# When the turning in layer 3, the loads of x and one normalization are issued in a four-layer graph network kernel

## The chip, the cores and the metric

The kernel runs on one core of one Trainium2 chip, as one launch. The metric is the device time in microseconds (us) of that launch; the times below are medians of several runs. The engines are called by their short names: PE is TensorE, DVE is VectorE, ACT is ScalarE, POOL is GpSimd and SP is SyncE. Each takes its own instructions from its own queue, in the order in which the program put them there.

## The reference, cut to what matters

There are 128 graphs of 64 nodes with 256 features each, and one 64x64 adjacency. Four layers follow each other, each on a normalized copy of x and each added back to x. All is float32.

```python
def reference(x, adj, ...):                    # x: 128 x 64 x 256
    # layer 0: two graph convolutions, then an LSTM over windows of 1, 2, 3 and 4 nodes
    h = max(layernorm(x), 0)
    h = relu(adj @ (h @ Wg0 + bg0)); h = relu(adj @ (h @ Wg1 + bg1))
    for p in (1, 2, 3, 4):
        h[:, p-1::p] = lstm_last(Wih[p-1], Whh[p-1], windows of p nodes of h)
    x = x + h
    # layer 1: attention with four heads under the mask of adj
    h = max(layernorm(x), 0); x = x + attention(h @ W, adj)
    # layer 2: adjacency, linear 256->512, batch norm, relu, linear 512->256, batch norm
    h = max(layernorm(x), 0); x = x + batchnorm(relu(batchnorm(A_hat @ h @ W1.T)) @ W2.T)
    # layer 3: three convolutions with adj * adj, 256 -> 512 -> 1024 -> 256
    h = max(layernorm(x), 0); w = adj * adj
    return x + w @ (relu(w @ (relu(w @ (h @ W1)) @ W2)) @ W3)
```

## The kernel before, in words

The 8192 tokens (a token is one node of one graph) are cut into 16 groups of 512. `xs[g]` is the residual x of group g with tokens on partitions: four tiles `x0` to `x3` that stay from the start, eight parts of the tiles `x_for_h0` and `x_for_h1` (groups 4 to 11) that take the room of two tiles of h when the LSTM has no more use for it, and four tiles for groups 12 to 15.

Products of matrices are done by a scheme with seven block products instead of eight. `sums` and `differences` (L206 and L218) make its operands, mostly on DVE. `seven` issues the seven products on PE: products 1, 5, 6 and 7 first, whose results ACT copies to p1 and p5 (L173, L174) and DVE adds to them (L176, L177); then products 2, 3 and 4, with the output blocks made by DVE (L185, L189) and one of them by POOL, the sum at L180.

**The LSTM** runs over windows of p nodes, for p = 1 to 4. For p = 4 the last pair of units is j = 2; there each step t = 1, 2, 3 is done for i = 0 and i = 1 by `next_step`, with two sets of gates (`gate_set`, the products at L560). `output` ends a step: tanh of the cell on ACT (L593), and a multiply with the output gate on DVE (L595 for the state, L601 in the last step, where the result goes back to h). Beside these steps h goes back to x, in pieces numbered by `slot = 2 t + i - 2`: `turn_nodes` transposes 32x32 blocks on DVE (L270) and puts them to DRAM tensors y with SP's queue (L275); `x_for` loads the input x of four groups (`load_x`, L58, SP); `add_turned` (L283) adds y to `xs[g]` with an accumulating transfer that POOL issues. Pieces for which there is no room in the LSTM are turned and added in the attention.

When step t = 3, i = 0 has been issued, the program normalizes `xs[0]` (`ln_relu`): statistics on DVE (L92, L94, L95), the inverse root on POOL (L96), the shift on DVE (L98) and four activations on ACT (L111). `transposed` then turns it with eight transposes on PE (L127), and `features` copies the result to `hT` (L294) and makes its differences (L298, L302, L303).

**The attention** goes over the groups one by one. In group g `queries_keys` makes q and k with the seven products (L872; the sum of k is L180 on POOL), `scores` are at L919, `add_output` multiplies on DVE (L980) and adds to x on POOL (L983), `normalized` prepares group g + 2 (L853 to L859), and `shifts_made[g]` is its last POOL instruction (L859) for group g + 1.

**Layer 3** goes over the groups too: `first_weights` (L1408), `second_mix` (L144, with copies L154), `second_weights` (L1444), `start` for the next group, `third_weights` (L1489), and `last_mix` (L1510) of the group before with its residual add (L1529). Beside them the output of layer 2, which is held feature by feature in `outs`, goes back to x: `normalize(g)` applies the second batch norm on ACT (L1280) or DVE (L1282), and `bring` takes groups in turn: the first eight are turned on PE (`to_residual`), the others by `turn_over`, with two transposes on DVE (L1317) and eight puts to DRAM by SP (L1321); `add_over` adds the DRAM tensor z to `xs[g]` with an accumulating transfer from POOL (L1330).

The order on each engine comes from the order in the program and from a list scheduler that may move independent work; `tc.issue_after(instruction)` ties what is issued inside it behind that instruction.

Of the kernel before, what the change touches and what calls it, by code (L numbers as in the profile page):

```python
# [10 lines left out]
ALU = mybir.AluOpType  # L11
# [9 lines left out]
NG = NTOK // GN  # L21
# [3 lines left out]
NK = PER  # L25
# [13 lines left out]
def adj_preln_kernel(ctx: ExitStack, tc: tile.TileContext, x_in, adj, vec, bg0, bg1,  # L39
                     wg0, wg1, wih, whh, wqkv, w1t, w2t, l3w1, l3w2, l3w3, out):  # L40
    nc = tc.nc
# [119 lines left out]

    HN = GN // 2

    def seven(products, banks, p1, p5, out, end, parts=lambda b: [b]):

        ps = banks  # L170
        for i, p in zip((1, 5, 6, 7), ps):
            products[i](p, True)
        nc.scalar.copy(p1, ps[0])  # L173
        copied = nc.scalar.copy(p5, ps[1])  # L174

        nc.vector.tensor_tensor(p1, p1, ps[2], ALU.add)  # L176
        added = nc.vector.tensor_tensor(p5, p5, ps[3], ALU.add)  # L177

        def finish():
            nc.gpsimd.tensor_tensor(out=out[1][1], in0=p1, in1=p5, op=ALU.add)  # L180
            end(1, 1, None)
            products[2](ps[0], False)
            end(0, 0, ps[0])
            products[3](ps[1], False)
            nc.vector.tensor_tensor(out[0][1], p1, ps[1], ALU.add)  # L185
            end(0, 1, None)
            products[4](ps[3], False)
            for to, p, q in zip(*(parts(b) for b in (out[1][0], p1, ps[3]))):
                last = nc.vector.tensor_tensor(to, p, q, ALU.add)  # L189
# [116 lines left out]
    with tc.tile_pool(name="lw", bufs=5) as lw:  # L306
# [220 lines left out]
        with tc.tile_pool(name="back", bufs=1, reuse_waits="tile") as back_pool, \  # L527
# [62 lines left out]
            def output(t, p, u, gate_o, th):  # L590

                x_of, cell, hid = u
                nc.scalar.activation(th, cell, AF.Tanh)  # L593
                if t < p - 1:
                    nc.vector.tensor_tensor(hid, gate_o, th, ALU.mult)  # L595
                else:
                    for blk in range(2):
                        o, h = (
                            v[:, :, blk, :].rearrange("p c (k b) -> p c k b", b=HB) for v in (gate_o, th)
                        )  # L600
                        nc.vector.tensor_tensor(x_of(t, blk), o, h, ALU.mult)  # L601

            behind = []

# [63 lines left out]
            def next_step(t, p, n, u, ws, last_sum=None):  # L668

                x_of, cell, hid = u  # L670
                tt = dp.tile([P, 4, 2, 256], F32, tag="diff", name="diff")
                ts = [tt[:, i, :, 0:n] for i in range(4)]
                wide = [d.rearrange("p c (k b) -> p c k b", b=HB) for d in ts]
                x1, x2 = (x_of(t, blk) for blk in range(2))
                h1, h2 = (hid[:, :, blk, :] for blk in range(2))
                nc.vector.tensor_tensor(wide[0], x2, x1, ALU.subtract)
                nc.vector.tensor_tensor(
                    wide[2], h2.rearrange("p c (k b) -> p c k b", b=HB), x2, ALU.subtract
                )
# [12 lines left out]
                output(t, p, u, gate_o, gate_g)  # L692

            def first_blocks(wi, room, behind=None):

# [28 lines left out]
            for p, nk in ((1, 8), (2, 8), (3, 7), (4, 8)):  # L724
# [7 lines left out]
                for j in range(0, len(units), 2):  # L732
# [22 lines left out]
                            nc.vector.tensor_tensor(wdiff, wqk[0][0], wqk[1][0], ALU.subtract)  # L755
                    for t in range(1, p):
                        for i, u in enumerate(two):
                            next_step(t, p, n, u, ws, last_sum if (j, t, i) == (0, 1, 0) else None)

                            if p == 4 and j == 2:  # L760
                                slot = 2 * t + i - 2
                            if p == 4 and j == 2 and t == p - 1:
                                for x_of_group in range(4 + 2 * i, 6 + 2 * i):
                                    add_turned(x_of_group)
                                if i == 0:
                                    x_for(1)
                            if p == 4 and j == 2 and t < p - 1:
                                if slot == 0:
                                    room = keep.tile([P, 2, TN, 2, 32], F32, tag="arena", name="turned")
                                for part in range(2 * slot, 2 * slot + 2):  # L770
                                    turn_nodes(
                                        part,
                                        room[:, part % 3] if part % 3 < 2 else back_pool.tile(
                                            [P, TN, 2, 32], F32, tag="hc", name="turned"
                                        ),
                                    )()
                                if slot == 2:
                                    x_for(0)
                                if slot > 1:
                                    for x_of_group in range(2 * slot - 4, 2 * slot - 2):  # L780
                                        add_turned(x_of_group)
                            if p == 4 and j == 2 and t == p - 1 and i == 0:

                                h = back_pool.tile([P, GT, D], F32, tag="hc", name="h")
                                ln_relu(xs[0], h)
                                hTs = keep.tile([P, 2, 2, GN], F32, tag="arena", name="hT")
                                hT = features(transposed(h))

# [54 lines left out]
    with tc.tile_pool(name="att", bufs=2, reuse_waits="tile") as ap_:  # L843
# [151 lines left out]
        for g in range(NG):  # L995
# [36 lines left out]
            if g == 1:  # L1032

                eT, turned = turn(e)
            if NK < g <= NG - NK:
                with tc.issue_after(shifts_made[g]):
                    add_turned(g + NK - 1)
            if g + 1 < NG:
                hT = features(transposed(h))
            if g == 0:  # L1040
# [268 lines left out]
    room = w_att[:, :, 512:1024]  # L1309
    turned_over = []  # L1310

    def turn_over(g):

        o = outs[g // 2][:, 2 * (g % 2) : 2 * (g % 2) + 2, :]
        y = turned_pool.tile([GN, D], F32, tag=f"z{g}", name=f"z{g}")
        for c in range(2):
            nc.vector.transpose(room[:, c], o[:, c, :])  # L1317
# [110 lines left out]
    def second_weights(m1, room):  # L1428
# [38 lines left out]
            end()  # L1467
        return h2, last

    def third_weights(h2, parts=lambda b: [b]):  # L1470


# [7 lines left out]
            )  # L1480
            for i in range(4)
        ]
        sums(nc.vector, *act[0], *act[1], *ss)

        def product(w, b):
            def issue(ps, first):
# [65 lines left out]
    for g in range(NG + 1):  # L1552
        if g == 0:
            bring(0, 3)
        if g < NG:

            m1 = arena(ar_right)
            h1, summed = first_weights(a, m1)
            if g == 0:
                with tc.issue_after(summed):  # L1560
                    finish_start()
            bring(3 if g == 0 else 1, 2 if g == 0 else 1)
        if s3 is not None:
            pss = [bank((P, 2, D)) for _ in range(2)]
            if g == NG:
# [14 lines left out]
        if g < NG:  # L1580
            h2, behind = second_weights(m1, h1)
            if g == 0:
                with tc.issue_after(behind):
                    for b, pss in later:
                        add_back(b, pss)
            bring(1, 1)
            if g + 1 < NG:
                a = start(g + 1, behind)
            if g == NG - 1:
                s3 = third_weights(h2, lambda b: [b[:, t] for t in range(2)])  # L1590
            else:
                s3 = third_weights(h2)


# [50 lines left out]
```

## Time and profile before

| | us |
|---|---|
| median of three runs | 2455.6 (2454.81 to 2458.61) |
| the profiled execution | 2455.04 |
| its span, first to last instruction | 2453.3 |
| PE busy | 2429.1 |
| DVE busy | 1538.6 |
| ACT busy | 1127.0 |
| POOL busy | 464.5 |

The time of an execution is a little longer than its span; every place in the trace is told in us from the span's start. PE, the busiest engine, stands still for 24.2 us of the span, and the granted clock of PE is 1.00 in the profile's record. The layers lie so: the convolutions of layer 0 to about 163, the LSTM to 1208, the attention to about 1425, layer 2 to about 1670, layer 3 to the end.

### The profile page before, as it was taken

The page shows a single profiled execution, that of the slowest core. Times are in us where ns is not written, and L with a number is a line of the kernel's source. Part 1 is how long each engine was busy: PE and PEld are TensorE (multiplying, and loading weights), DVE is VectorE, ACT ScalarE, POOL GpSimd, SP SyncE. Part 2 cuts the span into 40 slices and gives each one's busy share as a digit, 9 for nine tenths or more (in the row PEclk, how much of TensorE's full clock was granted, in tenths as well). Part 3 has the DMA queues.
Part 4 walks back from the last instruction along what each step waited for, and adds up shares of the span by engine and source line. Part 5 has one row for each costly group of instructions (what it writes and reads, how often), then busy time and mean ns, then how long its engine had stood idle before and what let it go on. Part 6 is the DMA issues. An engine that isn't in the chain of part 4 may idle for free.

```text
span 2453.3 us, 46571 instructions
## 1 busy us (share of the span) xinstructions
PE 2429.1 (99%) x19564; PEld 2072.5 (84%) x19564; DVE 1538.6 (63%) x2768; ACT 1127.0 (46%) x2026; POOL 464.5 (19%) x400
## 2 busy tenths in 40 slices
PE   9999999999999999999999999999999999999999
PEld 6678888889999998888888864487888898898888
DVE  6668866656566576585599886476655445454544
ACT  4557754444445343344455566564333323333332
POOL 4431211111111111122134331033111111111110
PEclk9999999999999999999999999999999999999999
DMA  3200000001000000173046410011322000000000
GB/s 128 93 2 1 1 18 1 1 1 35 1 1 1 1 1 1 18 128 75 14 88 120 79 34 1 1 61 23 64 48 42 10 10 19 10 10 10 18 10 18
DMA packets 161586, 73.20 MB, mean 30 GB/s; under 512 B 104416, under 2 KB 157792, under 8 KB 161376
## 3 DMA queue, kind: packets, MB, share of 16 engines
q1 hardware_dynamic: 147712, 56.82, 9.4%
q0 software_dynamic: 12672, 12.58, 3.4%
q8 instruction: 154, 2.52, 0.4%
q10 hardware_dynamic: 992, 0.82, 0.1%
q14 instruction: 56, 0.46, 0.1%
HBM read 40.84 MB, written 20.97 MB: 25 GB/s over the span
## 4 chain that ended last, share of the span: by engine, by line
PE 87%; DVE 7%; ACT 3%; issue 1%; POOL 1%; DMA 0%; SPq 0%; DVEq 0%; POOLq 0%; ACTq 0%
PE ps L560 40%; PE ps L1444 15%; PE ps L1489 8%; PE ps L822 4%; PE ps L144 4%; PE ps L872 3%; PE ps L1408 2%; PE ps L503 2%; PE ps L479 2%; PE ps L1201 2%; PE ps L1252 2%; PE ps L894 1%; ACT arena L229 1%; POOL arena L180 1%; PE ps L955 1%
## 5 line engine op out<-in xcount | busy, mean ns | idle before, releaser
L1444 PE MATMUL ps<-arena 128*128 128x256 f32 x1792 | 392.9, 380 | 2.7 <-DVE arena L206 1.4
L560 PE MATMUL ps<-diff,s 128*128 128x256 f32 (+1 forms) x1824 | 393.5, 371 | 0.9 <-DVE diff L680 0.9
L1444 PEld LDWEIGHTS ps<-arena 128*128 128x128 f32 x1792 | 338.0, 190 | 57.4 <-issue 6.9
L560 PEld LDWEIGHTS ps<-diff,s 128*128 128x128 f32 x1824 | 345.9, 190 | 33.8 <-issue 1.6
L574 ACT ACTIVATE gates<-gates,lbias 128x512 f32<-128x512 f32 (+5 forms) x426 | 244.3, 621 | 205.9 <-DVE gates L185 149.1
L180 POOL TENSOR_TENSOR gates<-p 128x512 f32<-128x512 f32 (+1 forms) x115 | 149.0, 1296 | 881.6 <-DVE p L177 830.8
L560 PE MATMUL ps<-h,w 128*128 128x256 f32 (+1 forms) x1028 | 241.0, 371 | 0.0
L560 PE MATMUL ps<-diff,w 128*128 128x256 f32 (+1 forms) x1040 | 238.8, 371 | 1.9 <-DVE p L177 1.9
L560 PEld LDWEIGHTS ps<-diff,w 128*128 128x128 f32 x1040 | 197.3, 190 | 20.5 <-DVE p L177 2.3
L560 PEld LDWEIGHTS ps<-h,w 128*128 128x128 f32 x1028 | 195.0, 190 | 19.2 <-issue 0.5
L574 ACT ACTIVATE gates<-ps,lbias 128x256 f32<-128x256 f32 (+3 forms) x213 | 91.6, 476 | 242.2 <-PE ps L560 242.1
L180 POOL TENSOR_TENSOR arena<-arena 128x256 f32<-128x256 f32 (+1 forms) x73 | 82.5, 1130 | 583.0 <-DVE arena L177 553.3
L229 ACT ACTIVATE arena<-arena 128x512 f32<-128x512 f32 (+1 forms) x160 | 88.7, 582 | 196.4 <-POOL arena L180 105.7
L1489 PE MATMUL ps<-arena 128*128 128x128 f32 x1280 | 149.9, 276 | 0.0
L185 DVE TENSOR_TENSOR gates<-p,ps 128x512 f32<-128x512 f32 (+1 forms) x115 | 76.2, 663 | 114.0 <-PE ps L560 113.8
L1489 PEld LDWEIGHTS ps<-arena 128*128 128x128 f32 x1280 | 145.6, 192 | 1.2 <-issue 0.2
L185 DVE TENSOR_TENSOR arena<-arena,ps 128x256 f32<-128x256 f32 (+1 forms) x73 | 43.5, 596 | 152.8 <-PE ps L1444 84.0
L560 PE MATMUL ps<-state,w 128*128 128x256 f32 (+1 forms) x512 | 116.1, 370 | 0.9 <-ACT p L173 0.8
L189 DVE TENSOR_TENSOR gates<-p,ps 128x512 f32<-128x512 f32 (+1 forms) x115 | 76.5, 666 | 64.4 <-PE ps L560 63.8
L176 DVE TENSOR_TENSOR p<-p,ps 128x512 f32<-128x512 f32 (+1 forms) x131 | 86.7, 662 | 47.5 <-PE ps L560 46.9
L560 PE MATMUL ps<-state,s 128*128 128x256 f32 (+1 forms) x512 | 115.8, 369 | 0.0
L822 PE MATMUL ps<-arena,w 128*128 128x512 f32 x256 | 114.3, 599 | 0.0
(207 smaller groups left out, 4016.6 us busy)
## 6 DMA issues: line engine op xcount, KB each, us to landing
x<-in_x SPq DMA_DIRECT2D x19, 512.0 KB, 4.7
y<-turned SPq DMA_DIRECT2D x64, 128.0 KB, 3.8
v<-vt SPq DMA_DIRECT2D x128, 64.0 KB, 2.2
w<-in_wih SPq DMA_DIRECT2D x4, 1024.0 KB, 8.0
x_for_h<-in_x SPq DMA_DIRECT2D x8, 512.0 KB, 7.0
x<-y POOLq DMA_DIRECT2D x8, 512.0 KB, 8.2
x_for_h<-y POOLq DMA_DIRECT2D x8, 512.0 KB, 6.5
z<-w SPq DMA_DIRECT2D x64, 64.0 KB, 2.0
```

Of the source, the lines that this page charges most:

```text
L144: last = nc.tensor.matmul(pss[b][half * 64 : half * 64 + 64, c, t, :], lhsT=src[rows, t, col : col + 64], rhs=a2[rows, :], start=True, sto ...
L176: nc.vector.tensor_tensor(p1, p1, ps[2], ALU.add)
L180: nc.gpsimd.tensor_tensor(out=out[1][1], in0=p1, in1=p5, op=ALU.add)
L185: nc.vector.tensor_tensor(out[0][1], p1, ps[1], ALU.add)
L189: last = nc.vector.tensor_tensor(to, p, q, ALU.add)
L229: nc.scalar.activation(o, o, func)
L560: nc.tensor.matmul(ps[:, r], lhsT=wc[:, j, :], rhs=bc, start=first and r == 0 and c == 0, stop=True, skip_group_check=True,)
L574: nc.scalar.activation(o, ps, func, bias=lbias[:, col : col + 1])
L822: nc.tensor.matmul(ps, lhsT=w1[:, c, m * P : (m + 1) * P], rhs=a[:, 2 + c, :], start=(c == 0), stop=(c == 1),)
L872: nc.tensor.matmul(ps[:, r, :], lhsT=w[:, r * P : (r + 1) * P], rhs=x, start=first and r == 0, stop=True, skip_group_check=True,)
L1444: nc.tensor.matmul(ps[:, r, :], lhsT=w[:, c, col : col + P], rhs=b[:, c, :], start=first and r == 0 and c == 0, stop=c == 1, skip_group_ch ...
L1489: nc.tensor.matmul(ps[:, t, :], lhsT=w[:, c, t * P : (t + 1) * P], rhs=b[:, c, :], start=first and t == 0 and c == 0, stop=c == 3, skip_gr ...
```

## The change

Four edits are made together.

1. In the LSTM's last pair of units, x's additions are spread: one group's addition in each of slots 2, 3 and 4 and two in slot 5, each tied behind POOL's last sum at L180. The loads of x for four groups each come in slots 3 and 4, behind all puts of y.
2. The normalization of `xs[0]` is tied behind the last multiply of step t = 3, i = 0 (`stepped`).
3. The additions for groups 5, 6 and 7 go to groups 1, 2 and 3 of the attention.
4. In layer 3 the two transposes of a group that is turned over, and the normalization of a later one, are tied behind the differences of `second_weights`, or behind the last sum of `third_weights`; `add_over` is tied behind POOL's last sum. The call of `bring` after `first_weights` stays for group 0 alone, and one after `third_weights` takes its place for the others.

`sums_on_pool` is the list of POOL's sums, to which `seven` appends; all else of `seven`, `add_turned`, `normalize` and `third_weights` is as before.

```diff
+    sums_on_pool = []
+    ADDED_BESIDE = ((), (), (0,), (1,), (2,), (3, 4))
+    def summed_last():
+        return sums_on_pool[-1]
...
         def finish():
-            nc.gpsimd.tensor_tensor(out=out[1][1], in0=p1, in1=p5, op=ALU.add)
+            sums_on_pool.append(
+                nc.gpsimd.tensor_tensor(out=out[1][1], in0=p1, in1=p5, op=ALU.add).ins
+            )
...
-                            if p == 4 and j == 2 and t == p - 1:
-                                for x_of_group in range(4 + 2 * i, 6 + 2 * i):
-                                    add_turned(x_of_group)
-                                if i == 0:
-                                    x_for(1)
-                            if p == 4 and j == 2 and t < p - 1:
...
-                                for part in range(2 * slot, 2 * slot + 2):
+                                for part in range(2 * slot, min(2 * slot + 2, 8)):
...
-                                if slot == 2:
-                                    x_for(0)
-                                if slot > 1:
-                                    for x_of_group in range(2 * slot - 4, 2 * slot - 2):
+                                for x_of_group in ADDED_BESIDE[slot]:
+                                    with tc.issue_after(summed_last()):
                                         add_turned(x_of_group)
+                                if slot > 2:
+                                    if slot < 5:
+                                        x_for(slot - 3)
                             if p == 4 and j == 2 and t == p - 1 and i == 0:
...
-                                ln_relu(xs[0], h)
+                                with tc.issue_after(stepped):
+                                    ln_relu(xs[0], h)
...
-            if NK < g <= NG - NK:
+            if 0 < g <= NG - NK:
                 with tc.issue_after(shifts_made[g]):
-                    add_turned(g + NK - 1)
+                    if g < 4:
+                        add_turned(g + NK)
+                    elif g > 4:
+                        add_turned(g + NK - 1)
...
-    def turn_over(g):
+    def turn_over(g, behind):
...
-        for c in range(2):
-            nc.vector.transpose(room[:, c], o[:, c, :])
+        with tc.issue_after(behind):
+            for c in range(2):
+                nc.vector.transpose(room[:, c], o[:, c, :])
...
-    def bring(n, ahead):
+    def bring(n, ahead, behind=None):
         nonlocal ready, brought
-        add_over()
         for _ in range(n):
+            if turned_over:
+                with tc.issue_after(summed_last()):
+                    add_over()
             if brought < ready:
-                (to_residual if brought < NG // 2 else turn_over)(brought)
+                if brought < NG // 2:
+                    to_residual(brought)
+                else:
+                    turn_over(brought, behind)
                 brought += 1
         for _ in range(ahead):
             if ready < NG:
-                normalize(ready, on_scalar=range(2 if ready < 5 else 1))
+                with tc.issue_after(behind) if behind else nullcontext():
+                    normalize(ready, on_scalar=range(2 if ready < 5 else 1))
                 ready += 1
...
-            bring(3 if g == 0 else 1, 2 if g == 0 else 1)
+            if g == 0:
+                bring(3, 2)
...
-            bring(1, 1)
+            bring(1, 1, behind)
...
                 s3 = third_weights(h2)
+                if g:
+                    bring(1, 1, third_summed)
```

More of the change, by code (lines that the diff above doesn't have):

```diff
@@ L594, in output @@
                 if t < p - 1:
-                    nc.vector.tensor_tensor(hid, gate_o, th, ALU.mult)
+                    last = nc.vector.tensor_tensor(hid, gate_o, th, ALU.mult)
                 else:
@@ L600, in output @@
                         )
-                        nc.vector.tensor_tensor(x_of(t, blk), o, h, ALU.mult)
+                        last = nc.vector.tensor_tensor(x_of(t, blk), o, h, ALU.mult)
+                return last.ins
             behind = []
@@ L691, in next_step @@
                 nc.vector.tensor_tensor(cell, cell, gate_i, ALU.add)
-                output(t, p, u, gate_o, gate_g)
+                return output(t, p, u, gate_o, gate_g)
             def first_blocks(wi, room, behind=None):
@@ L757, in adj_preln_kernel @@
                         for i, u in enumerate(two):
-                            next_step(t, p, n, u, ws, last_sum if (j, t, i) == (0, 1, 0) else None)
+                            stepped = next_step(
+                                t, p, n, u, ws, last_sum if (j, t, i) == (0, 1, 0) else None
+                            )
                             if p == 4 and j == 2:
                                 slot = 2 * t + i - 2
-                            if p == 4 and j == 2 and t == p - 1:
-                                for x_of_group in range(4 + 2 * i, 6 + 2 * i):
-                                    add_turned(x_of_group)
-                                if i == 0:
-                                    x_for(1)
-                            if p == 4 and j == 2 and t < p - 1:
                                 if slot == 0:
                                     room = keep.tile([P, 2, TN, 2, 32], F32, tag="arena", name="turned")
-                                for part in range(2 * slot, 2 * slot + 2):
+                                for part in range(2 * slot, min(2 * slot + 2, 8)):
                                     turn_nodes(
@@ L1468, in second_weights @@
         return h2, last
+    third_summed = None
     def third_weights(h2, parts=lambda b: [b]):
@@ L1482, in third_weights @@
         ]
-        sums(nc.vector, *act[0], *act[1], *ss)
+        nonlocal third_summed
+        third_summed = sums(nc.vector, *act[0], *act[1], *ss)
         def product(w, b):
```

## The prediction

> **What bounds the kernel now.** I read the busy times first, then TensorE's waits, then the timeline where those waits lie. Page, parts 1 and 4 (busy time; shares of the chain that ended last):
>
> ```profile
> PE 2429.1 (99%) x19564; PEld 2072.5 (84%) x19564; DVE 1538.6 (63%) x2768; ACT 1127.0 (46%) x2026; POOL 464.5 (19%) x400
> PE 87%; DVE 7%; ACT 3%; issue 1%; POOL 1%; DMA 0%; SPq 0%; DVEq 0%; POOLq 0%; ACTq 0%
> ```
>
> TensorE (PE) is the bound: idle for 2453.3 - 2429.1 = 24.2 us in all. The change alters no matmul and no order on PE, so it can win part of these 24.2 us, or add idle time to them. PE's waits (releaser: total, times, longest) and the timeline (start, us, engine, line, operation, [idle before it <- releaser]) at the three places that it touches:
>
> ```profile
> PE ps L560 <- DVE p L177: 1.9, 1, 1.9
> PE ps L919 <- POOL k L180: 1.8, 3, 0.6
> ...
> 1081.48 5.41 POOL L283 DMA_DIRECT2D x<-y  x4
> 1090.20 0.43 DVE L92 BATCH_NORM_STATS2 st<-x 128x6 f32<-128x256 f32 x1 [4.31 <-DMA x<-y]
> 1096.87 1.99 PE L560 MATMUL ps<-diff,w 128*128 128x256 f32 x8 [1.94 <-DVE p L177]
> ...
> 1181.58 1.89 PE L560 MATMUL ps<-diff,w 128*128 128x256 f32 x8
> 1183.31 1.04 PE L127 MATMUL ps<-ident,h 128*128 128x128 f32 x8
> 1184.18 1.89 PE L560 MATMUL ps<-h,w 128*128 128x256 f32 x8
> ```
>
> At 1090 VectorE (DVE) stands 4.31 us at the first statistics of x0, which wait for its accumulating transfer; the LSTM's adds queue behind, and PE loses 1.94 us. At 1183 the transposes of h (x0 normalized early, around 1100) stand on PE between the last product of step t=3, i=0 and the first of i=1, and PE does not stop. In layer 3 a turning transpose is in the way:
>
> ```profile
> 1739.89 0.71 DVE L1317 STREAM_TRANSPOSE w<-arena 128x512 f32<-128x512 f32 x1 [0.74 <-ACT arena L1280]
> 1741.78 3.69 PE L1444 MATMUL ps<-arena 128*128 128x256 f32 x16 [0.74 <-DVE arena L154]
> ```
>
> DVE waits for ScalarE's normalization, transposes, and so copies the mix (L154) late.
>
> **What the Trainium skill says.** "TensorE: Matmul & The Clock Gate", Part 2, step-by-step: "The MATMULs themselves stay in program order". The trace agrees: 1183.31 stands where the program has it. So a transpose that waits holds back everything behind it. Same page, Part 1, what's actually happening: after an idle window of about 3.4 us the array's clock halves until about 3.4 us of work have passed. The granted clock is 1.00 all through here, but at the span's start 14 matmuls of 128x128 took 3.35 us (239 ns each), while layer 3's L1489 of that width take 5.62/48 = 117 ns. "GPSIMD Engine Reference", 1. Specifications: the SBUF interfaces are shared with VectorE, with contention for DVE instructions with two SBUF inputs. The trace agrees (DVE L298: 0.69 us alone, 1.94 us under a GpSimd sum; shown below).
>
> **The change, part by part.** Lines are those of the kernel before.
>
> (a) End of the LSTM, the wait at 1090. The additions to x0 to x4 now go one by one behind GpSimd's (POOL's) sums of slots 2 to 5, and SyncE's loads of x4 to x7 pass behind the last eight puts of y. Each added transfer costs POOL about 0.85 to 1.3 us of issuing in gaps of 9 to 11 us (idle before L180); I take 0. x0 is added behind the second sum of t=2, i=0 (1130.9 in the timeline), and the statistics move to about 1190: the wait goes. Gain 1.9 us; bounds 1 and 1.94. Late next could be a transpose waiting for its put, but the puts now share the DMA engines with fewer transfers.
>
> (b) The normalization of x0 tied behind `stepped`. This is the term that decides. `stepped` is the last multiply of L601 in step t=3, i=0. The statistics, the inverse root, ScalarE's (ACT) four activations and then PE's eight transposes all come after it; the transposes keep their place in PE's queue, ahead of all products of step i=1. From PE's last product to h there is now one serial chain. Its first half is shown by step i=1, its second by a normalization in layer 3:
>
> ```profile
> 1208.56 0.69 DVE L189 TENSOR_TENSOR gates<-p,ps 128x512 f32<-128x512 f32 x1 [1.04 <-PE ps L560]
> 1213.76 1.29 DVE L601 TENSOR_TENSOR h<-gates 128x512 f32<-128x512 f32 x2 [1.18 <-ACT gates L593]
> ...
> 1746.27 1.40 DVE L92 BATCH_NORM_STATS2 st<-x 128x6 f32<-128x256 f32 x4
> 1749.49 2.08 ACT L111 ACTIVATE arena<-x,nmr,rstd 128x256 f32<-128x256 f32 x4 [3.40 <-DVE nmr L98]
> ```
>
> PE could go on at 1208.36 there, and L601 ended at 1215.05: 6.7 us. From statistics to the end of L111: 1751.57 - 1746.27 = 5.3 us. The new order puts one statistic of x1 between (0.34 us, most of the others beside POOL's root): 5.6. Six of the eight transposes run between the activations; the last two cost 2 x 0.13, with about 0.25 for the first weight load. h is thus complete at 1183.3 + 6.7 + 5.6 = 1195.6, and the next product starts at about 1196.1 instead of 1184.2: **11.9 us** of PE time, with nothing else in the queue to fill it. Bounds 11.0 (a quicker hand-over) and 12.6. Queued behind: all of step i=1. The copies of hT, its differences and x1's statistics then stand before L173 and L176, but those need PE's products, over 1.9 us later.
>
> (c) The clock after (b). Twelve us almost without matmuls are long enough for the page's throttle; 4 us at half rate cost 2.0 us. Bounds: 0 (the eight transposes keep it up) and 4 (the slow start lasted about 8 us). I take **2.0**.
>
> (d) Additions to x5, x6, x7 move into attention groups 1, 2, 3, behind `shifts_made`. POOL's new order in groups 2 and 3 is transfer, two output adds (L983), then the sum of k (L180), where before k came first. Groups 5 and 6 of the kernel before show both orders: windows (stretch, us, then busy times) of group 5 and group 6, and group 6's timeline:
>
> ```profile
> 1284.62:1298.47 13.85, 13.83 (x190) 11.92 (x189) 12.92 (x28) 7.98 (x15) 6.16 (x6) 1.00 0.74 137
> 1298.47:1313.56 15.09, 14.26 (x190) 12.10 (x189) 14.14 (x28) 8.18 (x15) 6.25 (x6) 1.00 0.78 157
> ...
> 1303.04 1.75 POOL L180 TENSOR_TENSOR k<-p 128x512 f32<-128x512 f32 x1
> 1303.41 1.94 DVE L298 TENSOR_TENSOR hT<-hT 128x512 f32<-128x512 f32 x1 [0.81 <-ACT hT L294]
> ```
>
> The late k falls under L298, and the group lasts 15.09 - 13.85 = 1.24 us longer. Twice: **2.5 us**. Group 1 has no output adds and k is ready 2.8 us before L919 needs it: 0. Bounds 0 and 2.6.
>
> (e) Layer 3. A group's period, between the starts of L1408 in the chain of waits, is 48.83, 48.37, 48.43 and 47.89 us for groups 1 to 4, which hold the turning, and 47.60 for most later ones: 3.1 us over the floor. Both transposes (2 x 0.70) and the normalization (0.5) now stand behind the differences, or behind the third sums, and no longer before L154. What queues behind them is L176/L177 of the second weights, whose products wait only after 14 us of others, and those of the third, needed at 1778.6 where they would end at about 1776.2. POOL's transfer follows its puts by half a group, so no wait is added there. Gain **3.1 us**; bounds 1.0 and 3.4. SyncE's 64 puts only change places.
>
> Sum: -1.9 + 11.9 + 2.0 + 2.5 - 3.1 = +11.4. The profiled execution took 2455.04 us (span 2453.3 and 1.74 around it), 0.56 below the median 2455.6 of three. 2455.04 + 11.4 = **2466.4 us**.
>
> **The rivals.** *Not slower: PE is not held at the transposes.* If h were ready by 1183.3 (an x0 normalized beside earlier steps, as before), (b) and (c) drop out: 2455.04 - 1.9 - 3.1 + 2.5 = 2452.5, or 2450.0 if (d) costs nothing as well. The point from which it decides: the chain in (b) would have to start 12 us earlier. For it: the kernel before did so. Against: the tie names the multiply itself, and DVE and ACT hold the chain in that order.
>
> *A heavier stall.* The clock stays low as long as at the start (+2) and ScalarE or DVE hand over late (+0.7): 2469.1. For it: the slow first 8 us. Against: step i=1 is dense, the start was not.
>
> *VectorE becomes the bound in layer 3.* The 1.9 us put ahead of L176 reach PE in the two turns of about four groups: 8 x 1.9 = 15.2 us and the 3.1 not won: 2484.7. Against: DVE is busy 24.2 of 48 us in such a group, and the slack named in (e).
>
> **How the numbers follow.** Forecast as worked out, 0.75; heavier stall 0.13; no stall 0.09; layer 3 bound 0.03. Low ends: 2455.04 + 11.0 + 0 + 0 - 1.94 - 3.4 = 2460.7. High ends: 12.6 + 4 + 2.6 - 1 - 1.0 = +17.2, 2472.2. The range 2460 to 2472 takes these in and leaves out the no-stall case and layer 3. A measurement tells about 0.2%, 4.9 us, from no change: slower by more 0.91, within 0.06 (most of the no-stall case), faster by more 0.03.
>
> **What would show each step.** (b) L127's first transposes waiting for ACT h L111, a total near 12 us in PE's waits, at about 1183; L92 behind L601. (c) L560's spacing near 430 ns for some 4 us afterwards. (a) No wait of PE on L177. (d) Groups 2 and 3 near 15.1 us, DVE L298 near 1.9. (e) Groups 1 to 4 of layer 3 at 47.6. The prediction is wrong if PE passes the transposes without an idle stretch of several us.

## The result, and the profile after

The changed kernel takes **2465.78 us** in the median of six runs (2465.19 to 2466.86); the kernel before takes 2455.11 beside it (2454.81 to 2458.61). The ratio is 1.0042, with a 95% interval of 1.0029 to 1.0055: slower by some 10.7 us. The prediction was 2466.4. The profiled execution has a span of 2464.0 us, 10.7 more than the 2453.3 of before.

Lines of the file have moved, so these are the same places under new numbers: the LSTM's products are L568 (L560 before), its last multiply L609 (L601), the sum on POOL L187 (L180), the second addition to p5 L183 (L177), the scores L926 (L919), the first weights of layer 3 L1419 (L1408). L92, L111 and L127 keep theirs. Parts 1 and 4 of the page of after:

```profile
PE 2431.4 (99%) x19564; PEld 2074.0 (84%) x19564; DVE 1544.5 (63%) x2768; ACT 1128.6 (46%) x2026; POOL 463.3 (19%) x400
PE 88%; DVE 7%; ACT 3%; POOL 1%; issue 1%; DMA 0%; DVEq 0%; POOLq 0%; ACTq 0%
```

PE executes the same 19564 matmuls and is busy 2.3 us longer, although no work was added to it: some of the products ran slower. It is idle for 2464.0 - 2431.4 = 32.6 us instead of 24.2. PE's waits in after, longest totals first (releaser: total, times, longest):

```profile
PE ps L127 <- ACT h L111: 11.0, 4, 10.5
PE ps L926 <- POOL k L187: 3.1, 5, 0.7
```

One wait of 10.5 us for the normalized x0 is new, the wait for the late k has grown from 1.8 to 3.1, and that of the LSTM's products for p is gone. The timeline of after at the new wait (start, us, engine, line, operation, [idle before it <- releaser]):

```profile
1179.69 1.89 PE L568 MATMUL ps<-diff,w 128*128 128x256 f32 x8
1186.82 1.29 DVE L609 TENSOR_TENSOR h<-gates 128x512 f32<-128x512 f32 x2 [1.18 <-ACT gates L601]
1188.04 1.40 DVE L92 BATCH_NORM_STATS2 st<-x 128x6 f32<-128x256 f32 x4
1191.45 2.07 ACT L111 ACTIVATE h<-x,nmr,rstd 128x256 f32<-128x256 f32 x4 [4.66 <-DVE nmr L98]
1192.10 2.16 PE L127 MATMUL ps<-ident,h 128*128 128x128 f32 x8 [10.52 <-ACT h L111]
1194.06 3.58 PE L568 MATMUL ps<-h,w 128*128 128x256 f32 x8
1197.47 5.35 PE L568 MATMUL ps<-diff,s 128*128 128x256 f32 x24
```

The chain stands there line by line: last product, multiply, statistics behind it, activations, transposes. The eight products at 1194.06 take 3.58 us where the eight at 1179.69 took 1.89. The windows of after (stretch, its length, then busy us of PE, PEld, DVE, ACT and POOL, then the granted clock, the DMA share and GB/s) say why; the last three are attention groups 2, 3 and 4:

```profile
1181.40:1194.06 12.66, 2.14 (x10) 1.35 (x9) 8.08 (x25) 4.58 (x8) 2.25 (x3) 0.60 0.22 34
1194.06:1197.47 3.41, 3.41 (x10) 2.69 (x9) 1.54 (x3) 1.07 (x2) 0.00 (x0) 0.50 0.00 0
...
1254.74:1269.92 15.18, 14.15 (x189) 11.94 (x188) 14.23 (x28) 8.07 (x15) 6.32 (x7) 1.00 0.62 103
1269.92:1285.11 15.19, 14.15 (x189) 11.94 (x188) 14.25 (x28) 8.06 (x15) 6.33 (x6) 1.00 0.65 111
1285.11:1298.96 13.85, 13.70 (x189) 11.73 (x188) 12.90 (x28) 7.83 (x15) 4.95 (x5) 1.00 0.49 103
```

The clock is 0.50 for 3.41 us after the wait. Groups 2 and 3 now last 15.2 us, where group 4, without an addition, lasts 13.85. POOL and DVE in group 2:

```profile
1259.40 1.75 POOL L187 TENSOR_TENSOR k<-p 128x512 f32<-128x512 f32 x1
1259.69 2.02 DVE L306 TENSOR_TENSOR hT<-hT 128x512 f32<-128x512 f32 x1 [0.81 <-ACT hT L302]
```

In layer 3, the chain of waits of after shows the starts of groups 1 to 4 (start, us, what):

```profile
1745.84 3.47 PE ps L1419 x16
1793.44 3.47 PE ps L1419 x16
1841.05 3.47 PE ps L1419 x16
1888.65 3.47 PE ps L1419 x16
```

Their distances are 47.60, 47.61 and 47.60 us; before they were 48.83, 48.37 and 48.43. In the second weights, PE's waits of before for the copies of the mix (L154, 0.7 on DVE and 0.6 on ACT) and for the operands' sums (L206, 1.4) are gone from the list of after.

Since PE's matmuls stand in one order in both traces, the start of each can be subtracted from that of its counterpart. The difference changes at few places, and these are the terms of the prediction (a plus is time lost):

| place (us) | term | predicted | measured |
|---|---|---|---|
| start of the span | none | 0 | +0.3 |
| 1094 to 1100 | (a) wait at 1090 | -1.9 | -2.2 |
| 1182 to 1194 | (b) wait at the transposes | +11.9 | +11.8 |
| 1194 to 1197 | (c) half clock | +2.0 | +1.7 |
| 1248 to 1285 | (d) late k in groups 2 and 3 | +2.5 | +2.8 |
| 1690 to the end | (e) layer 3 | -3.1 | -3.7 |
| sum | | +11.4 | +10.7 |

### The profile page after: what moved, and what is told of

Read it like the earlier page. It is cut to its first block, busy times and chain, and to the rows that moved or that the text cites. A ratio compares the mean times of both kernels' runs of the same rounds, so it can differ in the third digit from the quotient of the medians.

```text
span 2464.0 us, 46585 instructions
## 1 busy us (share of the span) xinstructions
PE 2431.4 (99%) x19564; PEld 2074.0 (84%) x19564; DVE 1544.5 (63%) x2768; ACT 1128.6 (46%) x2026; POOL 463.3 (19%) x400
## 4 chain that ended last, share of the span: by engine, by line
PE 88%; DVE 7%; ACT 3%; POOL 1%; issue 1%; DMA 0%; DVEq 0%; POOLq 0%; ACTq 0%
PE ps L568 41%; PE ps L1455 16%; PE ps L1503 8%; PE ps L829 4%; PE ps L144 4%; PE ps L1419 2%; PE ps L511 2%; PE ps L487 2%; PE ps L879 2%; PE ps L1211 2%; PE ps L1262 2%; PE ps L901 1%; ACT arena L237 1%; POOL arena L187 1%; DVE hT L306 1%
## 5 line engine op out<-in xcount | busy, mean ns | idle before, releaser
L568 PE MATMUL ps<-diff,s 128*128 128x256 f32 (+1 forms) x1824 | 393.5, 371 | 0.9 <-DVE diff L689 0.9
L568 PEld LDWEIGHTS ps<-diff,s 128*128 128x128 f32 x1824 | 346.1, 190 | 33.9 <-issue 1.6
L187 POOL TENSOR_TENSOR gates<-p 128x512 f32<-128x512 f32 (+1 forms) x115 | 149.2, 1297 | 892.5 <-DVE p L183 841.6
L568 PE MATMUL ps<-h,w 128*128 128x256 f32 (+1 forms) x1028 | 242.7, 373 | 0.0
L568 PE MATMUL ps<-diff,w 128*128 128x256 f32 (+1 forms) x1040 | 238.7, 370 | 0.0
L568 PEld LDWEIGHTS ps<-diff,w 128*128 128x128 f32 x1040 | 197.4, 190 | 18.2
L568 PEld LDWEIGHTS ps<-h,w 128*128 128x128 f32 x1028 | 196.2, 191 | 19.6 <-issue 0.5
L187 POOL TENSOR_TENSOR arena<-arena 128x256 f32<-128x256 f32 (+1 forms) x73 | 81.8, 1120 | 580.4 <-DVE arena L183 550.7
L568 PE MATMUL ps<-state,w 128*128 128x256 f32 (+1 forms) x512 | 116.1, 370 | 0.9 <-ACT p L179 0.8
L568 PE MATMUL ps<-state,s 128*128 128x256 f32 (+1 forms) x512 | 115.8, 369 | 0.0
```

Source lines behind the costliest of these rows:

```text
L568: nc.tensor.matmul(ps[:, r], lhsT=wc[:, j, :], rhs=bc, start=first and r == 0 and c == 0, stop=True, skip_group_check=True,)
```

## The experiments

The theory to test is that sum: one tie makes (b) and (c) and also wins (a), the moved additions make (d), and the edits of layer 3 win (e), each by itself. The rivals are that the long wait only covers others that would come elsewhere, that the half clock is a slow start of another kind, and that the gain in layer 3 depends on what came before it. The rivals named in the experiments are those of the expectation that stands above each. Line numbers shift by a few from kernel to kernel: the scores of L926 are L931 in busy_wait, the LSTM's products of L568 are L570 in later_transposes. The experiments ran in three comparisons, on three chips, and every ratio is to the runs of the kernel before on the same chip. Its medians there, against 2455.11 above, were 2456.02 us (for tie_alone, no_tie, adds_in_lstm and layer3_alone), 2457.04 (for tie_earlier, later_transposes, busy_wait and best_later) and 2455.55 (for busy_wait_64 and best_earlier).

### The tie alone, put into the kernel before (tie_alone)

The core of the edit; the other lines hand the last multiply on as `stepped`.

```diff
-                                ln_relu(xs[0], h)
+                                with tc.issue_after(stepped):
+                                    ln_relu(xs[0], h)
```

> The kernel before with only the tie of x0's normalization behind the last multiply of step t = 3, i = 0. My theory: the tie alone makes the stall at the transposes (+11.8) and the half clock (+1.7), and takes away the wait of the statistics for x0's transfer at 1090 (-2.2), since they are issued 100 us later: 2455.1 + 11.3 = 2466.4 us, between 2465 and 2468. Rival 1 (the stall needs the new order of additions and loads as well): about 2455, within 1. Rival 2 (the gain of 2.2 at 1090 comes from the spread additions and not from the later statistics): 2468.6, with the wait of PE L560 for DVE p L177 still there.

Measured: 2466.46 us, ratio 1.0039 (1.0027 to 1.0052), span 2464.7. PE's waits in this kernel begin with

```profile
PE ps L127 <- ACT h L111: 10.7, 2, 10.5
```

and its wait for L177 is gone. Against the trace of before the matmuls gain 2.2 us at 1094 and lose 13.6 from 1182 to 1197. So one edit holds (b) and (c), and (a) with them: the wait at 1090 goes because the statistics come 100 us later, whether x's additions are spread or not. Both rivals fall.

### The changed kernel without the tie (no_tie)

```diff
-                                with tc.issue_after(stepped):
-                                    ln_relu(xs[0], h)
+                                ln_relu(xs[0], h)
```

> The changed kernel without the tie of x0's normalization behind the last multiply of step t = 3, i = 0; all else as changed. The scheduler then puts the statistics of x0 (L92) beside an earlier step, while PE's order stays the same. My theory (the stall at the transposes is the whole loss, terms b and c): h is ready before PE comes to L127, PE does not stop there, and the 11.8 + 1.7 us go: 2465.8 - 13.5 = 2452.3 us, between 2451 and 2454. Rival 1 (the loss is spread over the other edits, and the long wait at L127 stands in for one that would come elsewhere): 2463 or more. Rival 2 (the statistics, placed earlier, wait for x0's accumulating transfer and hold the LSTM's adds as in the kernel before): about 2 us more than mine, 2454.3, with PE L568 waiting for DVE p L183 once.

Measured: 2455.99 us, ratio 0.9998 (0.999 to 1.0006), span 2453.3, as long as before. The long wait at L127 is gone, but the kernel is as fast as the one before, and not 2.8 us faster as was expected. The timeline of this kernel shows where these 2.8 us are (L859 are the statistics of x1):

```profile
1136.00 0.75 DVE L92 BATCH_NORM_STATS2 st<-x 128x6 f32<-128x256 f32 x2 [3.99 <-DMA x<-y]
1145.09 1.99 PE L568 MATMUL ps<-diff,w 128*128 128x256 f32 x8 [1.71 <-DVE p L183]
1162.09 0.75 DVE L859 BATCH_NORM_STATS2 st<-x 128x6 f32<-128x256 f32 x2 [3.93 <-DMA x<-y]
1170.03 1.99 PE L568 MATMUL ps<-diff,w 128*128 128x256 f32 x8 [0.50 <-DVE p L183]
```

The scheduler puts the statistics so early that they wait for the accumulating transfer of x0, and those of x1 for that of x1; the LSTM's adds queue behind them on DVE, and PE loses 2.0 and 0.8 us. This is rival 2, with a second wait that it did not name. The 2.2 us won at 1094 are thus given back, and with +2.7 in the attention and -3.3 in layer 3 the spans come out equal. The tie is thus not simply wrong: something has to hold these statistics back until the transfers have landed, only not until step t = 3, i = 0 ends.

### The tie one step earlier (tie_earlier)

```diff
+            stepped = None
...
-                            stepped = next_step(
+                            stepped_before, stepped = stepped, next_step(
...
-                                with tc.issue_after(stepped):
+                                with tc.issue_after(stepped_before):
```

> The changed kernel with x0's normalization tied behind the last multiply of the step before, t = 2, i = 1, about 14 us earlier; PE's order is the same. x0's transfer has landed by then (near 1136). My theory: h is ready before PE comes to L127, terms b and c go, and no statistic waits for a transfer; DVE does some 3 us of statistics ahead of that step's additions, which may hold PE by up to 1.5 us once: 2452.3 to 2453.8 us, most likely 2453. Rival (any tie to a multiply at a step's end leaves PE waiting at L127, since the chain and not the place of the tie sets h): 2460 or more.

Measured: 2452.70 us, ratio 0.9983 (0.9975 to 0.9990). In its timeline the transposes follow the last product without a stop:

```profile
1180.15 1.89 PE L568 MATMUL ps<-diff,w 128*128 128x256 f32 x8
1181.88 1.04 PE L127 MATMUL ps<-ident,h 128*128 128x128 f32 x8
```

The matmuls come 13.45 us earlier from there on than in the changed kernel, which is all of (b) and (c). The statistics that now stand among that step's additions on DVE cost PE nothing.

### The same tie, the transposes later on PE (later_transposes)

`next_step` gets an argument `between`, which it calls between its two sets of gates; the transposes are issued there for step t = 3, i = 1.

```diff
...
                 nc.vector.tensor_tensor(gate_i, gate_i, gate_g, ALU.mult)
+                if between is not None:
+                    between()
...
+                            def turn_h():
+                                nonlocal hT
+                                hT = features(transposed(h))
...
+                                turn_h if (p, j, t, i) == (4, 2, 3, 1) else None,
...
-                                hT = features(transposed(h))
```

> The changed kernel with the tie as it is, but the eight transposes and what follows them (features) issued between the two sets of gates of step t = 3, i = 1, about 12 us of PE's work later. x0's chain of statistics, root and activations starts where it starts in the changed kernel. My theory (the tie costs only because the transposes stand in PE's order ahead of step i = 1): PE has 11.5 us of products to do while the chain of 11.8 us runs, so it waits for under 1.5 us at L127 or not at all and keeps its clock: 2465.8 - 13.5 = 2452.3 us, up to 2454. Rival 1 (the late normalization itself holds up DVE and ACT, and so step i = 1): 2457 or more. Rival 2 (hT comes too late for the attention's first products): the wait shows up at L901 or L879 near 1208 instead, some 5 us, 2457.

Measured: 2453.60 us, ratio 0.9985 (0.9978 to 0.9991), on a chip where before took 2457.04. The timeline:

```profile
1187.32 1.40 DVE L92 BATCH_NORM_STATS2 st<-x 128x6 f32<-128x256 f32 x4
1194.21 0.77 PE L127 MATMUL ps<-ident,h 128*128 128x128 f32 x5 [0.16 <-ACT h L111]
1194.81 1.89 PE L570 MATMUL ps<-h,w 128*128 128x256 f32 x8
```

The statistics start at the same place behind the multiply as in the changed kernel, and yet PE loses only 1.2 us, in small stops between the transposes (12.3 of the 13.45 us are won there; the expectation of best_earlier below counts this loss as 0.9). So a late x0 costs little in itself: its price was the place of the transposes in PE's queue, ahead of 12 us of products that did not need them.

### PE kept busy in its wait (busy_wait and busy_wait_64)

```diff
+                                idle = bank((P, P))
+                                for _ in range(42):
+                                    nc.tensor.matmul(
+                                        idle, lhsT=ident, rhs=ident, start=True, stop=True
+                                    )
```

> The changed kernel with 42 products of the identity with itself (128x128, into a bank that nothing reads; the output is as before) on PE between the last product of step t = 3, i = 0 and the transposes, so that PE is busy for about 9.8 of the 10.5 us of its wait. The wait for the activations is the same, since DVE and ACT aren't touched. My theory (term c: the 1.7 us after the wait are the half clock that idleness brings): the products behind the transposes run at 216 ns each at once, the granted clock stays 1.00, and the time falls by 1.7: 2465.8 - 1.7 = 2464.1 us, although PE executes 9.8 us more. Rival 1 (the eight slow products are a slow start of data or weights after any wait): no change, 2465.8, and 430 ns each as in the changed kernel. Rival 2 (products of the identity don't count as activity for the throttle): also 2465.8, with a granted clock of 0.50.

Measured: 2468.65 us, ratio 1.0052 (1.0039 to 1.0065), span 2466.9, 2.9 us longer than the changed kernel's. The mechanism is right and the time wrong. Around the transposes the clock stays at 1.00 and step i = 1 comes 2.6 us earlier than in the changed kernel: 1.7 for the clock; the rest goes with PE's order, in which the transposes now stand mixed with the first products. But some 60 us later PE stands still, with no releaser. PE's waits in busy_wait, with the windows there below:

```profile
PE ps L931 <- issue: 5.5, 2, 3.0
```
```profile
1247.20:1250.60 3.40, 3.40 (x9) 2.72 (x9) 3.29 (x4) 0.00 (x0) 0.00 (x0) 0.51 0.65 95
```

After the first such stop, of 2.99 us up to 1246.86, the clock falls to one half for another 3.4 us. The trace's record of instruction transfers has one of 16 KB from 1244.5 to 1245.5, and PE goes on at 1246.9: this looks as if PE had run out of instructions. The second kernel of the pair changes only how many products are added:

```diff
-                                for _ in range(42):
+                                for m in 22 * [P] + 42 * [P // 2]:
                                     nc.tensor.matmul(
-                                        idle, lhsT=ident, rhs=ident, start=True, stop=True
+                                        idle[:m, :m], lhsT=ident[:m, :m], rhs=ident[:m, :m],
+                                        start=True, stop=True,
                                     )
```

> As busy_wait, but with 64 products instead of 42, 22 of 128x128 and 42 of 64x64, again about 9.8 us of PE's wait; the output is as before. In busy_wait the clock was kept and step i = 1 came 2.6 us earlier, but PE then stood still at about 1247, 1340 and 1449, where the trace names no releaser but only issue, and lost 5.3 us. What this run tells apart is whether that comes from the length of PE's instruction stream. My theory: PE's instructions arrive in blocks of fixed size (39128 matmuls and weight loads of the changed kernel came in some 154 blocks, so about 256 each), 42 products are two thirds of a block and move all later block boundaries to other work, 64 products (256 matmuls and weight loads, a whole block) move them by a full block and so leave them where they are: the waits on issue go, and the time is 2465.8 - 2.6 = 2463.2 us, between 2462.3 and 2464.5. Rival 1 (any added products bring these waits): 2467 or more, with PE L931 waiting on issue again. Rival 2 (the waits are a matter of chance in one execution): the median lies between, and the profile shows waits elsewhere.

Measured: 2464.97 us, ratio 1.0035 (1.0022 to 1.0047), span 2462.4. No wait on issue is left among PE's waits, and the matmuls come 2.05 us ahead of those of the changed kernel at 1196 and are still 1.9 ahead at the end. The median lies 0.5 us above the upper end expected. The windows of this kernel at the transposes:

```profile
1181.40:1192.00 10.60, 10.40 (x131) 10.09 (x129) 7.21 (x19) 3.07 (x5) 1.03 (x1) 1.00 0.29 46
1192.00:1196.00 4.00, 3.41 (x18) 2.70 (x19) 1.28 (x9) 2.98 (x7) 1.21 (x2) 1.00 0.00 0
```

PE does 10 us of needless work in the wait, keeps its full clock and comes out of it earlier: the clock term is shown. That the stops of busy_wait come from where PE's blocks of instructions end agrees with both runs (the traces have 154 of these transfers of 16 KB in the changed kernel and in busy_wait, 155 in busy_wait_64), but two lengths are few, and it is not shown further.

### The additions to x5, x6 and x7 beside the LSTM (adds_in_lstm)

```diff
-    ADDED_BESIDE = ((), (), (0,), (1,), (2,), (3, 4))
+    ADDED_BESIDE = ((), (), (0,), (1,), (2, 3), (4, 5, 6, 7))
...
-            if 0 < g <= NG - NK:
+            if NK < g <= NG - NK:
                 with tc.issue_after(shifts_made[g]):
-                    if g < 4:
-                        add_turned(g + NK)
-                    elif g > 4:
-                        add_turned(g + NK - 1)
+                    add_turned(g + NK - 1)
```

> The changed kernel, with the additions to x5, x6 and x7 beside the last LSTM steps (one more in slot 4, two more in slot 5) and no longer in attention groups 1 to 3, where POOL's sum of k stands before the output adds again. My theory (term d): groups 2 and 3 lose 1.3 us each less: 2465.8 - 2.7 = 2463.1 us, between 2462.4 and 2464, with both groups near 13.85 us. Rival 1 (the group's extra 1.3 us comes from the transfer's traffic or from the order of other work): 2465.5, groups near 15.2. Rival 2 (four additions in one slot of the LSTM delay POOL's sum or the transposes' puts): the gain in the groups is there but is lost before 1209 us, 2465 or more.

Measured: 2463.07 us, ratio 1.0026 (1.0017 to 1.0036). Windows of groups 2 and 3 in this kernel:

```profile
1254.76:1268.59 13.83, 13.69 (x189) 11.71 (x188) 12.89 (x28) 7.82 (x15) 4.92 (x5) 1.00 0.41 74
1268.59:1282.42 13.83, 13.82 (x190) 11.90 (x189) 12.90 (x28) 7.96 (x15) 4.92 (x5) 1.00 0.42 77
```

POOL is back at 4.9 us of work in a group, with k ahead of the output adds, and both groups last 13.83. In the four slots of the LSTM the three transfers cost nothing that can be seen. This run removes the transfers from the groups together with the order that they bring. The changed kernel itself separates the two: in its group 5 (1298.96 to 1312.81) POOL issues the same kind of transfer, but behind k and the output adds, and the group lasts 13.85. So what costs is the place of k behind the transfer and the output adds, and not the transfer as such.

### Layer 3 alone (layer3_alone)

The kernel before with edit 4 and `sums_on_pool`, and no other edit. Its core:

```diff
-        for c in range(2):
-            nc.vector.transpose(room[:, c], o[:, c, :])
+        with tc.issue_after(behind):
+            for c in range(2):
+                nc.vector.transpose(room[:, c], o[:, c, :])
...
+                    bring(1, 1, third_summed)
```

> The kernel before with only the edits of layer 3 (transposes and normalizations tied behind differences and third sums, the additions behind POOL's sums). My theory: the periods of groups 1 to 4 go from 48.83, 48.37, 48.43 and 47.89 to about 47.6 and nothing is given back: 2455.1 - 3.7 = 2451.4 us, between 2450.8 and 2452.5. Rival (part of the gain seen in layer 3 of the changed kernel comes from what the LSTM and the attention left in another order, or is given back in the last groups): 2453 to 2455.

Measured: 2452.08 us, ratio 0.9982 (0.9973 to 0.9990), span 2449.6, 3.7 below before. The groups start 47.60, 47.62, 47.77 and 47.90 us apart, and the matmuls gain 3.6 us between 1690 and the end, as in the changed kernel. The gain is layer 3's own, and the waits of the second weights for L154 and L206 are gone here too. How it divides among the transposes, the normalization and the additions was not tested. PE's wait of before at 1090 is still there, but shorter:

```profile
PE ps L567 <- DVE p L182: 1.5, 1, 1.5
```

### Both repairs together (best_later and best_earlier)

best_later is later_transposes with the additions of adds_in_lstm; best_earlier is tie_earlier with them. Against the changed kernel, best_earlier is:

```diff
-    ADDED_BESIDE = ((), (), (0,), (1,), (2,), (3, 4))
+    ADDED_BESIDE = ((), (), (0,), (1,), (2, 3), (4, 5, 6, 7))
...
+                            stepped_before, stepped = stepped, next_step(
...
+                                with tc.issue_after(stepped_before):
...
-            if 0 < g <= NG - NK:
+            if NK < g <= NG - NK:
...
```

> The same later transposes, together with the additions to x5, x6 and x7 beside the last LSTM steps (as in adds_in_lstm). If the terms add: 2465.8 - 13.5 - 2.8 = 2449.5 us, from 2449 to 2451.5, below the kernel before by 5.6 and below layer3_alone by about 2. Rival (the four additions of slot 5 and the late normalization share POOL and DVE in the same 12 us and get in each other's way): 2452 or more.

Measured: 2450.59 us, ratio 0.9974 (0.9964 to 0.9985).

> The tie to the step before (as tie_earlier) together with the additions to x5, x6 and x7 beside the last LSTM steps (as adds_in_lstm). If the terms add: 2465.8 - 13.45 - 2.8 = 2449.5 us, from 2449 to 2451, with a span about 0.6 us below that of best_later, where PE still lost 0.9 us at the transposes. Rival (the four additions of slot 5 delay POOL's root for x1 or the sums behind it): 2452 or more.

Measured: 2450.06 us, ratio 0.9975 (0.9966 to 0.9984). Here the terms add: against the matmuls of the changed kernel 13.45 us are won at the transposes and 2.8 in the attention. The span is no shorter than that of best_later in the profiled execution, because the clock was halved once more. Windows of best_earlier in layer 2, behind a stop of 1.08 us:

```profile
1452.00:1455.40 3.40, 3.40 (x5) 1.32 (x5) 3.24 (x12) 2.90 (x6) 1.80 (x3) 0.50 0.02 5
```

best_later has the same stop of 1.08 us there and kept its clock. By their ratios the two are alike, and both beat the kernel before by about 6 us.

## Why the prediction was right

**The deciding term, (b), was right in place and size.** The first half of the chain, from the last product to the end of the last multiply, was given as 6.7 us and took 1188.11 - 1181.41 = 6.7. The second, from the statistics to the last activation, was given as 5.6 and took 1193.52 - 1188.04 = 5.5. Taking the first from the same step for i = 1 and the second from a normalization in layer 3 worked, since both are the same instructions with little other work between them (the statistics of x1 that came between are in the 5.6). What the argument needed beside the durations, that PE keeps the transposes in their place, is shown by later_transposes: the same chain from the same place, with the transposes moved, costs 1.2 us. "TensorE: Matmul & The Clock Gate", Part 2, step-by-step, in the Trainium skill said so of PE, and the trace agrees.

**(c) was right in kind and a little large.** The eight products behind the wait took 3.41 us to the next one instead of 1.73: 1.7 us against 2.0. The prediction reckoned with 4 us at half rate; the slow products lasted 3.4. The range of 0 to 4 held it; busy_wait and busy_wait_64 show that idleness is its cause.

**(a) had the right sign and one wrong reason too many.** The prediction let the spread additions and the late statistics both stand behind the gain. tie_alone has all of it without spreading anything, and no_tie spreads them and loses it again. The later statistics are what wins. Measured 2.2, of which the stop is 1.94; the rest lies in the products at its two edges.

**(d) was read from the right pair of groups.** Groups 5 and 6 of before gave 1.24 us; groups 2 and 3 of after lost 1.3 and 1.4. In group 2 the sum of k on POOL takes 1.75 us, and DVE's L306 (L298 before) beside it 2.02, as the pair in group 6 of before had it. Group 1 lost nothing, as costed.

**(e) was mis-sized within its parts.** Groups 1 to 3 won what was counted. Group 4, which was to come down from 47.89 to 47.60, stayed at 47.89 (0.3 less). Groups that were not counted made up for it: group 0 won 0.25, two later ones 0.7 together, and group 5 lost 0.1. The upper bound of 3.4 was passed by 0.3. Why group 4 stayed is open.

The terms missed by 0.1 to 0.6 us each and by 1.0 together. That the sum is only 0.7 off is luck to the extent of 0.3 us, by which the start of the span, which is no term, differed.

Of the rivals, no stall at the transposes is refuted by 10.5 us of waiting in the trace, though tie_earlier shows that it was one step of the LSTM away. VectorE as a bound in layer 3 is refuted by the groups at 47.6. The heavier stall is refuted by the clock, full again 3.4 us after PE's first product, and by a chain that ran as fast as reckoned.

## What to carry to other kernels

A tie that delays a producer is paid where its consumer stands in an in-order queue: look at what is behind that consumer, not only at what is ahead of the producer, and then move either the tie or the consumer by as much as the chain lasts. A duration for an order that the profile doesn't show can be put together from two places that show its halves, if both run the same instructions undisturbed. When PE must wait for several us, add the slow clock behind the wait to its price.

## What the hardware showed beyond that

**The half clock comes in pieces of one length.** The trace's clock record has 0.50 for 13.65 us in the changed kernel (from 1183.8, while PE was still waiting, to 1197.5), for 10.24 us in adds_in_lstm at the same wait, and for 3.4 us in busy_wait, in best_earlier and, near 16 us, in tie_earlier, adds_in_lstm and layer3_alone: four, three and one times 3.41. The stretches at full clock between two pieces are whole multiples too (1266.35 us in the changed kernel is 371 times 3.413), so in these records the clock changes on a fixed grid. This bears on (c): at the same wait the half clock cost 1.7 us in the changed kernel, where it lasted 3.4 us past the first product, and 1.4 in adds_in_lstm, where it lasted 2.8. The piece in best_earlier followed a stop of only 1.08 us, which left the clock alone in best_later. "TensorE: Matmul & The Clock Gate", Part 1, what's actually happening, speaks of an idle window of about 3.4 us; as a length of the pieces this agrees, but as a least length of a stop it does not hold here, and the measurement decides. What else takes part in the decision is left open. In best_earlier and near 16 us PE ran many 64x64 products (L144) beside its short stops; whether these count for less was not tested.

**Much of the spread between runs goes with it.** Among the 82 runs of the kernel before beside the experiments, the 33 with a mean clock of 1.000 took 2454.6 to 2457.1 us, and the 15 with 0.998 took 2457.5 to 2460.5. Terms of 2 us are therefore read better from two traces, matmul by matmul, than from medians.

**Added matmuls can cost far from where they stand.** Forty-two products placed in a wait brought stops some 60 us and more behind it, in which PE waited for nothing but issue; sixty-four brought none.
